# Normalizing entering chunks per node, between two turns, in place of two averaging products

## The chip, the cores and the metric

The kernel runs on one core of one Trainium2 chip. The metric is the device time of one execution in microseconds (us), the median of several runs. TensorE (PE) multiplies matrices, VectorE (DVE) and ScalarE (ACT) work on elements, GpSimd (POOL) adds and moves data, and SyncE (SP) starts most of the transfers. Each engine works through its own queue in order and waits for the others by semaphores.

## The reference

Four graph layers run one after another on x of shape 8 x 2048 x 64 (batch, nodes, features), each with the same frame:

```python
h = jnp.maximum(_layernorm(x, axis=-1), 0.0)
x = x + layer(h, adj, ...)
```

The layer norm takes mean and variance over the 64 features of one node, without learned weights, with 1e-5 added to the variance. The change concerns layers 2 and 3:

```python
# layer 2: node 0 of h is overwritten with intervention_value, then three steps of
effects = jnp.einsum('nm,bmd->bnd', adj_matrix, v)
h = jax.nn.relu(jnp.einsum('bnk,dk->bnd', jnp.concatenate([v, effects], -1), W1) + b1)
v = jnp.einsum('bnk,dk->bnd', h, W2) + b2
# layer 3: products of x with I, A and 2AA - I, then weights that differ by node
out = jnp.einsum('bnki,nkio->bno', x_g, w) + b     # w, b made from a 16-wide embedding of the node
```

All four layers share the 2048 x 2048 adjacency matrix of zeros and ones.

## The kernel before

The eight batches form four pairs. A pair's state is a tile of 128 partitions (two batches with 64 features each) by 2048 nodes, held in four chunks of 512 nodes. This is the layout with features on the partitions. After layer 1 the state of each pair waits in DRAM (`x2_dram`). Then `layers23` works off layers 2 and 3 pair by pair, with the transposed adjacency matrix resident in SBUF (`aT`).

**A pair's work.** Layer 2 has three steps, each of four chunks. In each, `spread` (L2092) multiplies the features by one chunk of columns of the adjacency matrix: 16 row blocks, two matmuls each, since every factor is held as two rounded parts (hi and lo). In the third step each chunk is handed to `leave` (L2128), which adds the result to the state and already makes the normalized input of layer 3. Layer 3 spreads twice. In its last loop over the chunks (L2240), each chunk's spread gives y2, and then come the products with the weights that differ by node. For each of the four row tiles of the chunk and each of two halves of the weights (w), six matmuls fill two PSUM tiles, u0 and u1. DVE multiplies both by the embedding (L2269), adds (L2273) and folds (L2280); POOL folds further (L2281, L2282), adds the state (L2283), and SP stores the result (L2284).

**The next pair enters during that loop.** While chunk c of layer 3 is worked on, chunk c-1 of the next pair is loaded, normalized and written over the part of v that is no longer needed. In the last chunk (c = 3, LAST) two chunks enter: c = 2, and c = 3, which is kept in columns of `y1` until v is free. `enter` (L2115) does this. It calls `normed` (L2077), sets node 0 to the intervention value if c is 0, and calls `moved` (L2048). That makes the first weighted features of the next pair: four products `py`, then a rounded copy hi on ACT and the remainder lo on DVE (L2062, L2063).

**How `normed` works before.** Features lie on partitions, so their mean is a product: `kit.avg` is a 128 x 128 matrix with 1/64 in two diagonal blocks, and `mm(mean, kit.avg, src)` puts the mean of each node on all of its 64 partitions. DVE subtracts (L2082), ACT squares (L2083), a second product `var` averages the squares, ACT takes Ln and Exp with -0.5 (L2087, L2088), and DVE does maximum and multiplication (L2089). Both are float32 products of 512 columns.

**How `leave` works before.** It turns a chunk with four 128 x 128 transposes on PE (`kit.turn`), so that nodes lie on partitions. ACT copies the PSUM tile back over xp (L2140). The 64 features of a node then lie in a row, and a reduce on DVE gives their sum (L2144). DVE subtracts the mean (L2146), ACT squares (L2147), DVE reduces (L2148), ACT takes Ln and Exp of eight numbers per partition (L2149, L2150), and DVE does maximum and multiplication (L2151). The result vn is used turned. Later four more transposes (`tv`) turn it back, and ACT copies it into v (L2163).

**What sets the order of the work.** All of PE's instructions in these layers stand in program order. The program order is woven by a small planner, `Weave`: `enter` and the like are generators that yield an estimate, in microseconds, of the delay until their next part is due. `weave.passed(t)` is called after each piece of the main work and runs the parts that have come due. A row block of a spread counts 0.47, a group of six products of u counts 2.8. The other engines' orders come from the framework's scheduler, which keeps data dependences. [...]the tags acc, tp, u0 and u1 have two each, used in turn. The entering chunks use u0 and u1 for their products, so these alternate with the main products' tiles.

```python
if xn is not None:
    weave.start(enter(c - 1, after, xn, 0.2, ("u0", "u1")))
    if c == LAST:
        weave.start(enter(c, after, xl, 0.6, ("u0", "u1"), y1))
spread(acc, yn, c, True, every)
```

Of the kernel before, what the change touches and what calls it, by code (L numbers as in the profile page):

```python
# [8 lines left out]
FP = mybir.dt.float32  # L9
FR = mybir.dt.float32r  # L10
AF = mybir.ActivationFunctionType
OP = mybir.AluOpType
AX = mybir.AxisListType
# [3 lines left out]
P = 128  # L17
B, N, F = 8, 2048, 64
# [3 lines left out]
CW = 512  # L22
# [9 lines left out]
def cols(c, w=CW):  # L32
    return slice(c * w, (c + 1) * w)
# [603 lines left out]
class Kit:  # L637
# [97 lines left out]
    def mm(self, *args, **kw):  # L735

        one = self.nc.tensor.matmul(*args, **kw)  # L737
        if self.strict:
            self.tc.keep_in_program_order(one)
# [1267 lines left out]
def layers23(self, aT):  # L2007
    kit, x2_dram, x3_dram, out, ctx, fin, v = (
        self.kit, self.x2_dram, self.x3_dram, self.out, self.ctx, self.fin, self.v
    )  # L2010
    tc, nc, t, mm = kit.tc, kit.nc, kit.t, kit.mm
# [5 lines left out]
    sb = ctx.enter_context(tc.tile_pool(name="f_sb", bufs=2, reuse_waits="tile"))  # L2017
    ps = ctx.enter_context(tc.tile_pool(name="f_ps", bufs=2, space=PSUM, reuse_waits="tile"))
# [21 lines left out]
    def parts(lent):  # L2040

        if lent:
            return [sb.tile([P, 4, P], FR, tag=lent[0], name=n, bufs=lent[1]) for n in ("hi", "lo")]
        return self.parts()
# [3 lines left out]
    def moved(v, c, W, bias, lent=None):  # L2048

        py = ps.tile([P, 4, P], FP, tag="tp", name="py")  # L2050
        for k in range(4):
            m = 4 * c + k
            mm(py[:, k, :], v[:, m * P : (m + 1) * P], W, start=True, stop=True)
        return in_parts(py, bias, lent)

    def in_parts(py, bias=None, lent=None):
        hi, lo = parts(lent)
        if bias is not None:
            yb = fin.tile([P, 4, P], FP, tag="ca", name="yb")
            nc.vector.tensor_tensor(yb, py, bias[:, None, :].to_broadcast([P, 4, P]), op=OP.add)  # L2060
            py = yb
        nc.scalar.copy(hi, py)  # L2062
        nc.vector.tensor_tensor(lo, py, hi.bitcast(FP), op=OP.subtract)  # L2063
        return hi, lo
# [9 lines left out]
        nc.vector.tensor_tensor(lo, tp, hi.bitcast(FP), op=OP.subtract)  # L2074
        return hi, lo

    def normed(dst, src, tags, xc=None):  # L2077

        mean = ps.tile([P, CW], FP, tag=tags[0], name="mean")
        mm(mean, kit.avg, src, start=True, stop=True)  # L2080
        xc = fin.tile([P, CW], FP, tag="ca", name="xc") if xc is None else xc
        nc.vector.tensor_sub(xc, src, mean)  # L2082
        nc.scalar.activation(dst, xc, AF.Square)  # L2083
        yield 3.0
        var = ps.tile([P, CW], FP, tag=tags[1], name="var")
        mm(var, kit.avg, dst, start=True, stop=True)
        nc.scalar.activation(dst, var, AF.Ln, bias=kit.eps)  # L2087
        nc.scalar.activation(dst, dst, AF.Exp, scale=-0.5)  # L2088
        nc.vector.scalar_tensor_tensor(dst, xc, 0.0, dst, op0=OP.max, op1=OP.mult)  # L2089
        yield 3.0  # L2090

    def spread(acc, y, c, start, ms):  # L2092

# [14 lines left out]
    def load(dst, src, c):  # L2108
        nc.sync.dma_start(out=dst, in_=src[:, cols(c)])
        return dst  # L2110

    def chunk_of(src, c):
        return load(fin.tile([P, CW], FP, tag="x", name="xp"), src, c)

    def enter(c, y, xp, delay, tags, at=None):  # L2115

        yield delay
        src, k = (v, c) if at is None else (at, 1)
        yield from normed(src[:, cols(k)], xp, tags, at if at is None else at[:, cols(2)])
        if c == 0:  # L2120
            nc.vector.tensor_copy(v[:, 0:1], ivc)
        y[c] = moved(src, k, W1e, None)

    def carry(c, step, yn):
# [3 lines left out]
    def leave(p, c, xp, yn):  # L2128

        yield 1.8 if c == LAST else 2.3  # L2130
        pv = ps.tile([P, CW], FP, tag="tp", name="pv")
        mm(pv, W2, v[:, cols(c)], start=True, stop=True)
        nc.vector.scalar_tensor_tensor(xp, pv, b2c, xp, op0=OP.add, op1=OP.add)
        bq = load(sb.tile([P, CW], FP, tag="pr", name="bq", bufs=3), kit.bias_dram, c)
        yield 1.8

        tx = ps.tile([P, 4, P], FP, tag="u0", name="tx")
        for k in range(4):
            kit.turn(tx[:, k, :], xp[:, k * P : (k + 1) * P])
        nc.scalar.copy(xp, tx.rearrange("p k n -> p (k n)"))  # L2140
        groups = lambda a: a.rearrange("p (g f) -> p g f", f=F)
        spans = lambda a: a[:, :, None].to_broadcast([P, 8, F])
        st = sb.tile([P, 2, 8], FP, tag="st", name="st")
        nc.vector.tensor_reduce(st[:, 0], groups(xp), AX.X, OP.add)  # L2144
        vn = fin.tile([P, CW], FP, tag="ca", name="vn")
        nc.vector.scalar_tensor_tensor(groups(vn), spans(st[:, 0]), -1.0 / F, groups(xp), op0=OP.mult, op1=OP.add)  # L2146
        nc.scalar.activation(v[:, cols(c)], vn, AF.Square)  # L2147
        nc.vector.tensor_reduce(st[:, 1], groups(v[:, cols(c)]), AX.X, OP.add)  # L2148
        nc.scalar.activation(st[:, 1], st[:, 1], AF.Ln, bias=kit.eps, scale=1.0 / F)  # L2149
        nc.scalar.activation(st[:, 1], st[:, 1], AF.Exp, scale=-0.5)  # L2150
        nc.vector.scalar_tensor_tensor(groups(vn), groups(vn), 0.0, spans(st[:, 1]), op0=OP.max, op1=OP.mult)  # L2151
        hi, lo = parts(LENT[c])
        flat = lambda a: a.rearrange("p k n -> p (k n)")
        nc.scalar.copy(flat(hi), vn)
        nc.vector.tensor_tensor(flat(lo), vn, flat(hi).bitcast(FP), op=OP.subtract)
        yn[c] = hi, lo
        nc.gpsimd.tensor_add(bq, bq, xp)  # L2157
        nc.sync.dma_start(out=x3_dram[p, :, cols(c)], in_=bq)
        yield 7.0
        tv = ps.tile([P, 4, P], FP, tag="u1", name="tv")  # L2160
        for k in range(4):
            kit.turn(tv[:, k, :], vn[:, k * P : (k + 1) * P])
        nc.scalar.copy(v[:, cols(c)], flat(tv))  # L2163

    def again(y1, c, yn):
        yield 1.4
# [22 lines left out]
    for p in range(NP):  # L2189
        for step in range(3):  # L2190
# [3 lines left out]
            for c in range(NCW):  # L2194
                if step == 0 or c % 2 == 0:
                    accs = [ps.tile([P, CW], FP, tag="acc", name="acc") for d in range(2 if step else 1)]
                acc = accs[c % 2 if step else 0]
                if step < 2:
                    got = raw(2)
                else:  # L2200
                    xp = chunk_of(x2_dram[p], c)
                if step == 0:
                    mm(acc, W1v, v[:, cols(c)], start=True, stop=False)
                    weave.passed(0.93)
                    spread(acc, y, c, False, every)
                elif c % 2 == 0:
                    spread(acc, y, c, True, range(0, 8))
                    quarters(accs, Wvc, c)
                    spread(acc, y, c, False, range(8, NT))
                else:  # L2210
                    spread(acc, y, c, False, every)
                b = b1c if step else b1
                if step < 2 and c % 2:
                    for h in range(2):
                        nc.scalar.activation(v[half(1 - h), cols(c)], acc[half(h)], AF.Relu, bias=b[half(h)])
                else:
                    nc.scalar.activation(v[:, cols(c)], acc, AF.Relu, bias=b)
                if step < 2:
                    check(got)
                weave.start(carry(c, step, yn) if step < 2 else leave(p, c, xp, yn))  # L2220
# [19 lines left out]
        for c in range(NCW):  # L2240
            xr = chunk_of(x3_dram[p], c)
            acc = ps.tile([P, CW], FP, tag="acc", name="acc")
# [4 lines that stand above are left out]
# [7 lines left out]
            for k in range(4):  # L2254
# [3 lines left out]
                for w in range(2):  # L2258
                    u = [ps.tile([P, 8, F], FP, tag=f"u{h}", name=f"u{h}") for h in range(2)]
                    for kk, src in enumerate((v[:, ns], y1[:, ns], y2[:, ks])):  # L2260
                        for h in range(2):
# [3 lines left out]
                                start=kk == 0, stop=kk == 2,  # L2265
                            )
                    for h in range(2):
                        a = sb.tile([P, 8, F], FP, tag="pr", name="pr", bufs=3)
# [125 lines left out]
```

## Time and profile before

| | us |
|---|---|
| median of 3 runs (1881.08 to 1883.15) | 1881.71 |
| the profiled execution | 1880.27 |
| its span, first to last instruction | 1878.1 |
| PE busy (98% of the span) | 1840.7 |
| DVE busy (63%) | 1174.5 |
| ACT busy (25%) | 463.1 |
| POOL busy (17%) | 311.7 |

The TensorE clock granted to the core was 0.996 of full speed. PE, DVE, ACT, POOL and SP are the engines, PEld is PE's loading of weights. A line of the timeline gives start, duration, engine, line of the kernel, operation, output <- inputs, shapes and the number of merged instructions; in brackets stands how long the engine was idle before, and what ended that. A float32 matmul shows as two records, so one mean product is x2 and the four products py are x8. Transposes carry line L744, and all other matmuls here L737, since two helpers issue them. The chain of work that ended last follows the end of the program back, at each step to what released it. The three changes of pair lie at 980 to 1076, 1246 to 1343 and 1513 to 1609 us in the span.

### The profile page before, as it was taken

What the parts mean: (1) busy time and instruction counts of PE and PEld (TensorE: products, weight loads), DVE (VectorE), ACT (ScalarE), POOL (GpSimd) and SP (SyncE); (2) the same over time, 40 slices, a digit from 0 to 9 for tenths busy, and PEclk for the clock granted to TensorE, in tenths of its full rate; (3) what the DMA queues carried; (4) which work ended last, traced back from release to release, by engine and by line L of the source; (5) the groups of instructions that cost most, each with busy time, mean ns of one, the idle gap of its engine ahead of it and who ended that gap; (6) DMA issues with size and microseconds to landing.
All of it is one profiled execution on the core that took longest, in us unless ns stands there. A gap on an engine that the chain in (4) does not pass through costs nothing.

```text
span 1878.1 us, 26150 instructions
## 1 busy us (share of the span) xinstructions
PE 1840.7 (98%) x10364; PEld 1146.9 (61%) x10364; DVE 1174.5 (63%) x1843; ACT 463.1 (25%) x1048; POOL 311.7 (17%) x435
## 2 busy tenths in 40 slices
PE   8999999899999999999999999999999999999997
PEld 7877767443333333577765577855677755777653
DVE  7766699789999999932446732357523275524465
ACT  5422455572222221121301112200112101113000
POOL 4211387220000000000111200012100021101122
PEclk9999999999999999999999999999999999999999
DMA  7666395383222222142101022101122011121000
GB/s 205 186 185 207 103 284 144 107 208 79 54 61 52 63 57 57 46 99 67 51 13 28 22 69 62 34 23 26 43 62 62 12 30 28 54 65 51 5 20 12
DMA packets 86372, 142.60 MB, mean 76 GB/s; under 512 B 33800, under 2 KB 34056, under 8 KB 83568
## 3 DMA queue, kind: packets, MB, share of 16 engines
q1 hardware_dynamic: 64976, 80.64, 14.8%
q0 software_dynamic: 21040, 56.98, 12.4%
q10 hardware_dynamic: 224, 3.22, 0.5%
q8 instruction: 83, 1.36, 0.3%
q14 instruction: 49, 0.40, 0.1%
HBM read 106.85 MB, written 37.09 MB: 77 GB/s over the span
## 4 chain that ended last, share of the span: by engine, by line
PE 50%; issue 10%; DMA 2%; POOL 2%; DVE 1%; POOLq 0%; ACT 0%; SPq 0%; DVEq 0%
PE acc L737 31%; PE u L737 14%; PE py L737 2%; PE pv L737 1%; POOL fold L2281 1%; PE var L737 1%; PE mean L737 1%; DMA xd<-e 0%; DMA W3f<-in_L_gnn_weight 0%; DMA den<-d_dram 0%; PE tx L744 0%; POOL ot L2282 0%; PE tv L744 0%; PE tp L744 0%; DVE pt L1807 0%
## 5 line engine op out<-in xcount | busy, mean ns | idle before, releaser
L737 PE MATMUL acc<-aT,parts 128*128 128x512 f32 x1664 | 441.3, 409 | 0.0
L737 PEld LDWEIGHTS acc<-aT,parts 128*128 128x128 f32 x1664 | 306.6, 188 | 97.7 <-issue 39.2
L737 PE MATMUL o<-pt,hS 128*32 128x512 f32 x2048 | 247.1, 593 | 2.0 <-DVE pt L632 1.2
L737 PE MATMUL u<-W3f,y 64*128 64x512 f32 x1024 | 241.3, 589 | 0.0
L2269 DVE TENSOR_TENSOR pr<-u,embf 128x512 f32<-128x512 f32 x256 | 170.6, 687 | 109.8 <-PE u L737 103.1
L1807 DVE SCALAR_TENSOR_TENSOR pt<-R,wd,aT 128x1024 f32<-128x1024 f32 x188 | 230.0, 1276 | 8.5 <-DMA R<-r_dram 5.2
L737 PEld LDWEIGHTS u<-W3f,y 64*128 64x128 f32 x1024 | 100.0, 187 | 119.8 <-issue 119.8
L737 PEld LDWEIGHTS o<-pt,hS 128*32 128x32 f32 x2048 | 79.1, 110 | 143.8 <-issue 112.8
L737 PE MATMUL dn<-pt,vd 128*32 128x512 f32 x1024 | 134.9, 593 | 0.0
L737 PE MATMUL u<-W3f,v 64*128 64x512 f32 x512 | 133.0, 596 | 0.0
L2281 POOL TENSOR_TENSOR fold<-fold 128x256 f32<-128x256 f32 x64 | 47.8, 746 | 495.8 <-DVE fold L2280 495.8
L2060 DVE TENSOR_TENSOR yb<-py,cb_f 128x512 f32<-128x512 f32 x32 | 22.1, 691 | 157.9 <-PE py L737 157.9
L1106 PE MATMUL acc<-at,Y 128*128 128x512 f32 x384 | 101.7, 405 | 0.3 <-ACT ev L1136 0.2
L737 PE MATMUL acc<-aTl,parts 128*128 128x512 f32 x384 | 99.7, 398 | 0.0
L2157 POOL TENSOR_TENSOR bq<-bq,xp 128x512 f32<-128x512 f32 x16 | 20.7, 1293 | 421.9 <-ACT xp L2140 421.9
L2273 DVE TENSOR_TENSOR pr<-pr 128x512 f32<-128x512 f32 x128 | 88.0, 688 | 2.2
L737 PEld LDWEIGHTS u<-W3f,v 64*128 64x128 f32 x512 | 56.5, 186 | 49.6 <-issue 36.3
L1807 DVE SCALAR_TENSOR_TENSOR pt<-R,wd,aTl 128x1024 f32<-128x1024 f32 x64 | 79.3, 1280 | 8.6 <-PE dn L737 3.9
L737 PEld LDWEIGHTS dn<-pt,vd 128*32 128x32 f32 x1024 | 40.7, 110 | 67.7 <-issue 49.2
L737 PEld LDWEIGHTS acc<-aTl,parts 128*128 128x128 f32 x384 | 71.5, 188 | 16.2
L1106 PEld LDWEIGHTS acc<-at,Y 128*128 128x128 f32 x384 | 68.5, 188 | 14.1 <-issue 0.8
L2074 DVE TENSOR_TENSOR parts<-tp,parts 128x512 fp32r<-128x512 f32 x16 | 11.1, 692 | 85.3 <-ACT parts L2073 85.3
(374 smaller groups left out, 2683.0 us busy)
## 6 DMA issues: line engine op xcount, KB each, us to landing
at<-in_adjT POOLq DMA_DIRECT2D x32, 512.0 KB, 4.6
raw<-in_adjT SPq DMA_DIRECT2D x64, 256.0 KB, 3.3
aT<-in_adjT POOLq DMA_DIRECT2D x12, 1024.0 KB, 7.5
xp<-xd SPq DMA_DIRECT2D x45, 256.0 KB, 2.9
R<-r_dram SPq DMA_DIRECT2D x14, 512.0 KB, 3.8
hhi<-hi_dram POOLq DMA_DIRECT2D x18, 235.1 KB, 4.3
hlo<-lo_dram POOLq DMA_DIRECT2D x18, 235.1 KB, 4.4
hi_dram<-hi SPq DMA_DIRECT2D x16, 264.0 KB, 3.1
```

The costliest lines, as they stand in the source:

```text
L737: one = self.nc.tensor.matmul(*args, **kw)
L1106: mm(acc[p], Y[h][:, m, p, :], at[:, k, :], start=m + h == 0, stop=m == NT - 1 and h == 1)
L1807: V.scalar_tensor_tensor(pt, R, w, a.bitcast(FP), op0=OP.max, op1=OP.mult)
L2060: nc.vector.tensor_tensor(yb, py, bias[:, None, :].to_broadcast([P, 4, P]), op=OP.add)
L2074: nc.vector.tensor_tensor(lo, tp, hi.bitcast(FP), op=OP.subtract)
L2157: nc.gpsimd.tensor_add(bq, bq, xp)
L2269: nc.vector.tensor_tensor(a, u[h], emb[:, i, 8 * w : 8 * w + 8, None].to_broadcast([P, 8, F]), op=OP.mult)
L2273: nc.vector.tensor_add(pr[h], pr[h], a)
L2281: nc.gpsimd.tensor_add(fold[:, :, 0:2, :], fold[:, :, 0:2, :], fold[:, :, 2:4, :])
```

## The change

The body of `leave` that turns and normalizes is moved into `normed`, and the turning back into `back`, both plain functions. `leave` calls them in place of the old lines, with the same instructions. `enter` calls them too, in place of the old `normed` with its two products.

```diff
-    def normed(dst, src, tags, xc=None):
-
-        mean = ps.tile([P, CW], FP, tag=tags[0], name="mean")
-        mm(mean, kit.avg, src, start=True, stop=True)
-        xc = fin.tile([P, CW], FP, tag="ca", name="xc") if xc is None else xc
-        nc.vector.tensor_sub(xc, src, mean)
-        nc.scalar.activation(dst, xc, AF.Square)
-        yield 3.0
-        var = ps.tile([P, CW], FP, tag=tags[1], name="var")
-        mm(var, kit.avg, dst, start=True, stop=True)
-        nc.scalar.activation(dst, var, AF.Ln, bias=kit.eps)
-        nc.scalar.activation(dst, dst, AF.Exp, scale=-0.5)
-        nc.vector.scalar_tensor_tensor(dst, xc, 0.0, dst, op0=OP.max, op1=OP.mult)
-        yield 3.0
+    def normed(xp, tag, vn, q):
+
+        tx = ps.tile([P, 4, P], FP, tag=tag, name="tx")
+        for k in range(4):
+            kit.turn(tx[:, k, :], xp[:, k * P : (k + 1) * P])
+        nc.scalar.copy(xp, tx.rearrange("p k n -> p (k n)"))
...
+        nc.vector.tensor_reduce(st[:, 0], groups(xp), AX.X, OP.add)
+        nc.vector.scalar_tensor_tensor(groups(vn), spans(st[:, 0]), -1.0 / F, groups(xp), op0=OP.mult, op1=OP.add)
+        nc.scalar.activation(q, vn, AF.Square)
+        nc.vector.tensor_reduce(st[:, 1], groups(q), AX.X, OP.add)
+        nc.scalar.activation(st[:, 1], st[:, 1], AF.Ln, bias=kit.eps, scale=1.0 / F)
+        nc.scalar.activation(st[:, 1], st[:, 1], AF.Exp, scale=-0.5)
+        nc.vector.scalar_tensor_tensor(groups(vn), groups(vn), 0.0, spans(st[:, 1]), op0=OP.max, op1=OP.mult)
+
+    def back(vn, dst, tag):
+
+        tv = ps.tile([P, 4, P], FP, tag=tag, name="tv")
+        for k in range(4):
+            kit.turn(tv[:, k, :], vn[:, k * P : (k + 1) * P])
+        nc.scalar.copy(dst, tv.rearrange("p k n -> p (k n)"))
...
     def enter(c, y, xp, delay, tags, at=None):
 
         yield delay
         src, k = (v, c) if at is None else (at, 1)
-        yield from normed(src[:, cols(k)], xp, tags, at if at is None else at[:, cols(2)])
+        vn = fin.tile([P, CW], FP, tag="ca", name="vn") if at is None else at[:, cols(2)]
+        normed(xp, tags[0], vn, src[:, cols(k)])
+        yield 7.0
+        back(vn, src[:, cols(k)], tags[1])
         if c == 0:
             nc.vector.tensor_copy(v[:, 0:1], ivc)
+        yield 1.4
         y[c] = moved(src, k, W1e, None)
```

The delays of `enter` change with it: before, 3.0 to the second product and 3.0 to `moved`; now 7.0 to the turning back and 1.4 to `moved`. In PE's order this puts tx where mean stood, removes var, puts the first tv behind the last row block of the spread, and puts py behind the first six products of u, where it stood ahead of the spread's last row block (or, for the second entry in LAST, behind it). In LAST the second entry's tv follows the first one's py, and its py follows the second six products.

More of the change, by code (lines that the diff above doesn't have):

```diff
@@ L2075, in turned @@
         return hi, lo
-    def normed(dst, src, tags, xc=None):
-        mean = ps.tile([P, CW], FP, tag=tags[0], name="mean")
-        mm(mean, kit.avg, src, start=True, stop=True)
-        xc = fin.tile([P, CW], FP, tag="ca", name="xc") if xc is None else xc
-        nc.vector.tensor_sub(xc, src, mean)
-        nc.scalar.activation(dst, xc, AF.Square)
-        yield 3.0
-        var = ps.tile([P, CW], FP, tag=tags[1], name="var")
-        mm(var, kit.avg, dst, start=True, stop=True)
-        nc.scalar.activation(dst, var, AF.Ln, bias=kit.eps)
-        nc.scalar.activation(dst, dst, AF.Exp, scale=-0.5)
-        nc.vector.scalar_tensor_tensor(dst, xc, 0.0, dst, op0=OP.max, op1=OP.mult)
-        yield 3.0
+    def normed(xp, tag, vn, q):
[3 more added lines that the diff above has]
+        nc.scalar.copy(xp, tx.rearrange("p k n -> p (k n)"))
+        groups = lambda a: a.rearrange("p (g f) -> p g f", f=F)
+        spans = lambda a: a[:, :, None].to_broadcast([P, 8, F])
+        st = sb.tile([P, 2, 8], FP, tag="st", name="st")
+        nc.vector.tensor_reduce(st[:, 0], groups(xp), AX.X, OP.add)
[10 more added lines that the diff above has]
+        nc.scalar.copy(dst, tv.rearrange("p k n -> p (k n)"))
     def spread(acc, y, c, start, ms):
@@ L2135, in leave @@
         yield 1.8
[L2137 to L2144, printed above, removed]
-        vn = fin.tile([P, CW], FP, tag="ca", name="vn")
[L2146 to L2151, printed above, removed]
+        vn = fin.tile([P, CW], FP, tag="ca", name="vn")
+        normed(xp, "u0", vn, v[:, cols(c)])
         hi, lo = parts(LENT[c])
@@ L2159, in leave @@
         yield 7.0
[L2160 to L2163, printed above, removed]
+        back(vn, v[:, cols(c)], "u1")
     def again(y1, c, yn):
```

## The prediction

> **What bounds the kernel now.** I read the profile's first part, then the chain of work that ended last, then the timeline of the entering chunks. The first part says that TensorE is busy all the time:
>
> ```profile
> PE 1840.7 (98%) x10364; PEld 1146.9 (61%) x10364; DVE 1174.5 (63%) x1843; ACT 463.1 (25%) x1048; POOL 311.7 (17%) x435
> ```
>
> Busy time alone proves little here, because a matmul lasts 409 ns by its record and the next one starts 232 ns later. The chain says more: from 976 us on, its long pieces are PE's own (acc, u, py, var, mean) and its issue time, with short tails of POOL (fold 1.2% of it). So in layers 2 and 3 a microsecond of PE slots is a microsecond of the end, as long as no operand is late. The slots are read as distances between starts. The timeline on PE has the entering chunk c=2 of the first pair, the LAST chunk (c=3, where two chunks enter), and two chunks of the last pair, in which nothing enters:
>
> ```profile
> 1011.65 0.73 PE L737 MATMUL acc<-aT,parts 128*128 128x512 f32 x2
> 1012.22 1.02 PE L737 MATMUL mean<-xp,avg_f 128*128 128x512 f32 x2
> ...
> 1016.28 1.06 PE L737 MATMUL var<-v,avg_f 128*128 128x512 f32 x2
> ...
> 1020.40 1.05 PE L737 MATMUL py<-W1e_f,v 128*128 128x128 f32 x8
> ...
> 1021.86 1.13 PE L737 MATMUL u<-W3f,v 64*128 64x512 f32 x4
> ...
> 1042.66 0.73 PE L737 MATMUL acc<-aT,parts 128*128 128x512 f32 x2
> ...
> 1076.24 1.13 PE L737 MATMUL acc<-v,W1v_f 128*128 128x512 f32 x2
> ...
> 1750.58 1.55 PE L737 MATMUL acc<-aT,parts 128*128 128x512 f32 x6
> ...
> 1779.29 5.74 PE L737 MATMUL acc<-aT,parts 128*128 128x512 f32 x24
> ...
> 1786.83 1.13 PE L737 MATMUL u<-W3f,v 64*128 64x512 f32 x4
> ...
> 1807.63 5.78 PE L737 MATMUL acc<-aT,parts 128*128 128x512 f32 x24
> ```
>
> A chunk with no guest takes 1807.63 - 1779.29 = 28.34 us (28.38 the next one): I take 28.36. With one guest it takes 1042.66 - 1011.65 = 31.01 us, so **one entering chunk costs 2.66 us** (31.02 - 28.36, c=1 having 31.02). LAST takes 1076.24 - 1042.66 = 33.58, so **two cost 5.21 us**. The other two pair changes repeat this (31.04 and 33.57 in the third). Of 2.66, py is 0.89 by the chain, so mean and var together are 1.77. One turn of a chunk (four transposes) is priced by the chunk from 1750.58 to 1779.29, which holds one (tp): 28.71 - 28.36 = **0.35 us**.
>
> The new chain has not run in these places, but it runs in the leaving chunks. From DVE, ACT and POOL on the timeline there:
>
> ```profile
> 897.00 0.69 DVE L2144 TENSOR_REDUCE st<-xp 128x8 f32<-128x512 f32 x1 [2.16 <-ACT xp L2140]
> 897.05 1.29 POOL L2157 TENSOR_TENSOR bq<-bq,xp 128x512 f32<-128x512 f32 x1 [81.79 <-ACT xp L2140]
> 897.72 1.17 DVE L2146 SCALAR_TENSOR_TENSOR vn<-st,xp 128x512 f32<-128x512 f32 x1
> 898.98 0.63 ACT L2147 ACTIVATE v<-vn 128x512 f32<-128x512 f32 x1 [2.02 <-DVE vn L2146]
> 899.64 0.69 DVE L2148 TENSOR_REDUCE st<-v 128x8 f32<-128x512 f32 x1 [0.76 <-ACT v L2147]
> 900.37 0.30 ACT L2149 ACTIVATE st<-st,eps_f 128x8 f32<-128x8 f32 x1
> 900.70 0.21 ACT L2150 ACTIVATE st<-st 128x8 f32<-128x8 f32 x1
> 900.94 0.69 DVE L2151 SCALAR_TENSOR_TENSOR vn<-vn,st 128x512 f32<-128x512 f32 x1 [0.61 <-ACT st L2150]
> ```
>
> From the first reduce to the end of vn this takes 4.63 us. And where DVE stands when an entering chunk begins (c=1, whose spread starts on PE at 980.63):
>
> ```profile
> 983.19 0.68 DVE L2273 TENSOR_TENSOR pr<-pr 128x512 f32<-128x512 f32 x1
> 983.79 0.68 DVE L2082 TENSOR_TENSOR xc<-xp,mean 128x512 f32<-128x512 f32 x1
> 984.39 0.42 DVE L2280 TENSOR_TENSOR fold<-pr 128x256 f32<-128x256 f32 x1
> 984.89 0.73 POOL L2281 TENSOR_TENSOR fold<-fold 128x256 f32<-128x256 f32 x1 [3.82 <-DVE fold L2280]
> ```
>
> DVE is still busy with the products of the chunk before for 3.2 us. The guest's first operation on DVE gets its turn 3.16 us after the spread began.
>
> **What the Trainium skill says.** SBUF — State Buffer, "Who interferes with whom": a VectorE instruction with two SBUF inputs contends with a GpSimd instruction that reads SBUF, and whichever started first keeps the shared ports for its whole length. The trace agrees with this: L2146 takes 1.17 us where L2151, of the same shape and also with two SBUF inputs, takes 0.69; POOL's bq add ran until 898.34, which is 0.62 into L2146, and 0.55 remain. All 16 of L2146 have this neighbour. VectorE: DVE Perf Modes, "The perf-mode tier table": tensor_reduce has only the 1x mode; the trace has 0.69 us for 512 elements, as dear as an add. TensorE: Matmul & The Clock Gate, "Part 4: PE-mode transpose": a 128x128 transpose lasts about 275 ns in a kernel; the records here say 272, but four of them hold up the stream only 0.35 us, so I use the spacing.
>
> **The change, part by part.** There are 12 entering chunks: three changes of pair, each with c=0 and 1 entering one at a time and c=2 and 3 together in LAST.
>
> Removed: mean and var, 1.77 us of PE in a single entry, subtraction and last multiply on DVE (0.68, 0.69), Square, Ln and Exp on ACT (0.63, 0.69, 0.63). Added: tx and tv on PE, 2 x 0.35 = 0.70; two copies of 0.59 and two tiny activations on ACT, which is busy for 25% of the span; two reduces on DVE. In the built program the order of SP and POOL is unchanged.
>
> Moved: py. It stood in the spread, two matmuls from its end; now it stands behind the first six products of u. There PE goes from products on half the rows to a full-array product and back. The first group of six takes 2.68 us after a spread and 2.57 later, and the last takes 2.67, so each crossing costs 0.10. py in the new place is 0.89 + 0.20 = 1.09. Its lower bound is 0.89 (the crossing hides behind weight loads). A single entry thus costs 0.70 + 1.09 = 1.79 in place of 2.66: **0.87 saved**. LAST costs 1.40 + 2.18 = 3.58 in place of 5.21: **1.63 saved** (its second tv shares py's crossing).
>
> New wait: tv stands right behind the spread and needs vn; every product of u is queued behind it, and DVE's multiplications behind those. PE gets there at 7.54 - 0.10 + 0.35 = 7.79 us after the spread began (7.54 is 1786.83 - 1779.29). DVE: reduce at 3.16 (in xc's place), fold at 3.76, L2146's subtraction at 4.09 (an add followed a fold 0.33 after its start). POOL's fold begins at 4.26 at the earliest, as in the fence, so the subtraction has the ports first and lasts 0.69. Then by the steps of the leaving chunk: Square 4.87, reduce 5.53, Ln 6.26, Exp 6.59, multiply 6.83 to 7.52. **0.27 before PE needs it: no wait.** If it lasts 1.17 all the same, vn is ready at 8.00 and PE waits 0.21.
>
> In LAST the two guests interleave on DVE: subtraction 4.09 to 4.78, second reduce to 5.38, second subtraction behind POOL's pushed-back fold (5.51) to 6.10, Square of the second on ACT to 6.8 ahead of the first's Ln, two reduces to 7.52, first vn 7.55 to 8.24. PE arrives at 7.44 + 0.70 = 8.14: a wait of **0.10**. With both subtractions at 1.17 vn comes at about 9.20: 1.06. The second tv also takes the u1 bank that alternates with the first products': 0.05.
>
> Late next, at no cost: lo of the entering chunk (0.69 on DVE) now lies among the products. In the single entry it falls into DVE's idle 1.29 us before the second group of products; in LAST, the second py's 1.09 on PE gives DVE the time. If that cover is gone, each costs up to 0.69. The freed xp buffer comes 0.9 us later, and its next load has a whole u stage of 20.8 us.
>
> Sum per pair change: 2 x 0.87 + 1.63 - 0.10 - 0.05 = 3.22; times 3 = **9.7 us**. The profiled execution took 1880.27 (span 1878.1 and 2.2 around it), which gives 1870.6; against the median of 1881.71 it gives **1872.0**. With turns at 0.44 (in the leaving chunk of the fence four transposes and six matmuls of 0.232 fill 1.83), 24 x 0.09 = 2.2 is lost; with py at 0.89, 12 x 0.20 = 2.4 is won.
>
> **The rivals.**
> - *The vn chain is late.* L2146 is slow by itself or POOL gets in first. For it: all 16 records say 1.17, never less. Against: the multiply L2151, of the same kind, takes 0.69 with POOL still. Waits of 0.21, 0.21 and 1.06 replace 0.10: 2 x 0.66 + 0.52 = 1.84, times 3 = 5.5; **1876.2**.
> - *lo is uncovered.* DVE needs 4.8 us of PE's 5.15 in each row tile, and waits on it only 0.35. If 12 times 0.69 came through, 8.3 would be given back: **1880.3**, no change. Against: py itself gives PE's side 1.09 each time.
> - *POOL's whole train goes first* (slower). POOL has three operations in a row there, 0.73 + 0.46 + 0.46, to 6.06. If the subtraction stands behind all of them, it ends at 6.61, vn at 9.35, in LAST at about 10.13; waits of 1.56, 1.56 and 1.99 against 3.32 saved: +1.79 per pair change, +5.4: **1887.1**. It decides if DVE's subtraction starts over 0.17 later than I put it, and it is a loss once the three waits pass 3.32. Against: DVE issues ahead, while POOL must be told that the fold is done.
>
> That the products stay is ruled out: the built order has no mean and var there.
>
> **How the numbers follow.** Forecast 0.58, late chain 0.24, lo 0.10, POOL first 0.08. The range runs from the cheap py (1869.6) to past the late chain with dearer turns (1876.2 + 1.7): 1869.6 to 1877.9, leaving out 0.18. Faster by over 0.2% (3.8 us, about what a measurement of this kernel can tell from no change) means below 1877.9: the first two, 0.82; within it, lo: 0.10; slower: 0.08.
>
> **What would show it.** Single-entry chunks of 30.15 us from spread to spread and LAST of 32.1; tx and tv of 0.35 each; the subtraction at 0.69 in entries and 1.17 in exits; POOL's fold lengthened instead; no PE wait before tv in single entries. It is wrong if PE stands before tv for over 0.3 us, if a gap opens in the u stage behind DVE, or if py's crossing is dearer than 0.2.

## The result, and the profile after

The median is 1875.83 us (1873.88 to 1877.00, seven runs) against 1882.46 for the kernel before (1880.53 to 1883.37, seven runs): a ratio of **0.9964 [0.9955, 0.9973]**, 6.6 us less. The forecast was 9.7 less. The profiled execution took 1875.95 (span 1874.1); the one before took 1880.27.

The first part of the page looks as it did, with TensorE busy all the time:

```profile
PE 1836.8 (98%) x10412; PEld 1150.6 (61%) x10412; DVE 1189.9 (63%) x1867; ACT 466.5 (25%) x1072; POOL 316.1 (17%) x435
```

The timeline of the kernel after on PE, from the spread of c=1 in the first pair to the end of LAST (start, length, engine, line, operation):

```profile
981.83 0.73 PE L737 MATMUL acc<-aT,parts 128*128 128x512 f32 x2
982.40 0.60 PE L744 MATMUL tx<-ident_f,xp 128*128 128x128 f32 x4
982.75 5.29 PE L737 MATMUL acc<-aT,parts 128*128 128x512 f32 x22
987.87 2.03 PE L737 MATMUL acc<-aTl,parts 128*128 128x512 f32 x8
989.74 0.60 PE L744 MATMUL tv<-ident_f,vn 128*128 128x128 f32 x4
990.27 1.13 PE L737 MATMUL u<-W3f,v 64*128 64x512 f32 x4
...
993.05 1.16 PE L737 MATMUL py<-W1e_f,v 128*128 128x128 f32 x8
994.13 1.13 PE L737 MATMUL u<-W3f,v 64*128 64x512 f32 x4
...
996.81 1.02 PE L737 MATMUL u<-W3f,v 64*128 64x512 f32 x4
...
1012.37 0.74 PE L737 MATMUL acc<-aT,parts 128*128 128x512 f32 x2
...
1042.91 0.73 PE L737 MATMUL acc<-aT,parts 128*128 128x512 f32 x2
...
1051.77 1.13 PE L737 MATMUL u<-W3f,v 64*128 64x512 f32 x4
...
1054.55 1.16 PE L737 MATMUL py<-W1e_f,v 128*128 128x128 f32 x8
1055.55 0.60 PE L744 MATMUL tv<-ident_f,y 128*128 128x128 f32 x4
1056.08 1.13 PE L737 MATMUL u<-W3f,v 64*128 64x512 f32 x4
...
1075.60 1.13 PE L737 MATMUL acc<-v,W1v_f 128*128 128x512 f32 x2
```

A chunk with one guest takes 30.54 us in place of 31.02, LAST 32.69 in place of 33.58. The whole stretch, from the first entering spread of a pair change to the products with W1v, took 95.61, 95.68 and 95.64 before; now it takes 93.77, 94.13 and 93.76. **Together that is 5.27 us less**, and this is the effect of the change as the traces show it: all that follows the first entering spread outside the three stretches takes 610.6 us in both. The medians say 6.6 with an interval of 5.1 to 8.5, which holds 5.27; whether the other 1.3 is more than scatter is not shown. The time ahead of the first entering spread scatters by more than that: it begins anywhere from 978.9 to 986.5 us in the profiles of this study (980.63 before, 981.83 after). So I compare stretches below, and medians beside them.

The new chain of the same guest, on DVE, ACT and POOL:

```profile
984.99 0.68 DVE L2086 TENSOR_REDUCE st<-xp 128x8 f32<-128x512 f32 x1
985.59 0.41 DVE L2277 TENSOR_TENSOR fold<-pr 128x256 f32<-128x256 f32 x1
985.92 0.68 DVE L2087 SCALAR_TENSOR_TENSOR vn<-st,xp 128x512 f32<-128x512 f32 x1
986.08 1.12 POOL L2278 TENSOR_TENSOR fold<-fold 128x256 f32<-128x256 f32 x1 [3.83 <-DVE fold L2277]
...
988.60 0.69 DVE L2092 SCALAR_TENSOR_TENSOR vn<-vn,st 128x512 f32<-128x512 f32 x1 [0.61 <-ACT st L2091]
989.51 0.59 PEld L744 LDWEIGHTS tv<-ident_f,vn 128*128 128x128 f32 x4
989.74 0.60 PE L744 MATMUL tv<-ident_f,vn 128*128 128x128 f32 x4
```

Counted from the spread's start at 981.83: reduce at 3.16, subtraction at 4.09 with 0.68 us, vn done at 7.46. PE starts tv at 7.91, with no idle time noted before it.

### The profile page after: what moved, and what is told of

It is laid out like the page before. It is cut to its first block, busy times and chain, and to the rows that moved or that the text cites. A ratio compares the mean times of both kernels' runs of the same rounds, so it can differ in the third digit from the quotient of the medians.

```text
span 1874.1 us, 26303 instructions
## 1 busy us (share of the span) xinstructions
PE 1836.8 (98%) x10412; PEld 1150.6 (61%) x10412; DVE 1189.9 (63%) x1867; ACT 466.5 (25%) x1072; POOL 316.1 (17%) x435
## 3 DMA queue, kind: packets, MB, share of 16 engines
q8 instruction: 84, 1.38, 0.3%
## 4 chain that ended last, share of the span: by engine, by line
PE 49%; issue 10%; DMA 2%; POOL 2%; DVE 1%; POOLq 0%; ACT 0%; SPq 0%; DVEq 0%
PE acc L737 31%; PE u L737 14%; PE py L737 2%; PE pv L737 1%; PE tx L744 1%; PE tv L744 1%; POOL fold L2278 1%; DMA xd<-e 0%; DMA den<-d_dram 0%; DMA W3f<-in_L_gnn_weight 0%; PE tp L744 0%; DMA d_dram<-ds 0%; POOL ot L2279 0%; DVE pt L1807 0%; POOL ot L2280 0%
## 5 line engine op out<-in xcount | busy, mean ns | idle before, releaser
L737 PE MATMUL acc<-aT,parts 128*128 128x512 f32 x1664 | 430.7, 404 | 0.0
L2082 ACT COPY xp<-tx 128x512 f32<-128x512 f32 x25 | 14.7, 588 | 203.3 <-PE tx L744 203.3
```

## The experiments

Edits are against the kernel after, unless it says otherwise. A ratio is to the kernel before, timed beside each run. "Stretch" is the mean of the three pair changes (95.65 before, 93.89 after); "chunks" are the three of the first pair change: the two single entries, then LAST (31.02, 31.01 and 33.58 before; 30.54, 30.54 and 32.69 after). A "crossing" is a change of PE between products on half the rows (u) and products on the full array.

**Is py dear because it stands among the products of u?** Two runs ask this from both sides. The first puts py of the kernel after into the spread of the next chunk:

```diff
         back(vn, src[:, cols(k)], tags[1])
...
-        yield 1.4
+        yield 23.0
         y[c] = moved(src, k, W1e, None)
```

> The changed kernel, with py of a single entry moved on from among the products of u into the next chunk's spread, and both py of LAST to the end of its products. If the shortfall is the crossing (py costs 1.30 us of PE among the products, 0.89 in a spread), a single-entry chunk falls from 30.54 to about 30.1 us counted with the py that moves on, LAST by 0.5 to 0.9, and the time is 3 to 5 us below the changed kernel's: ratio to the kernel before 0.994 to 0.995 in place of 0.9964. If the shortfall is a late vn, py's place doesn't matter and the ratio stays at 0.9964. If it is DVE's lo among the products, the time falls too, but gaps before u, and not py's own slot, vanish in the trace.

Measured: 1875.69, 0.9962 [0.9947, 0.9976]; stretch 93.49; chunks 29.22, 30.15 and 34.11. The second single takes 30.15 with the first one's py in its spread, against 30.54 with its own among u, so py is 0.4 cheaper there. LAST lost it again, and the 3 to 5 us that I had expected below the kernel after did not come. LAST now holds three py: the second single's in its spread, and its own two at the pair's end (1074.92 to 1076.81). Without the one that is not its own (some 0.92) it takes 33.19 against 32.69. The timeline of this run, behind the first six products of LAST, shows why:

```profile
1055.26 0.66 PE L744 MATMUL tv<-ident_f,y 128*128 128x128 f32 x4
1055.36 1.29 DVE L2266 TENSOR_TENSOR pr<-u,embf 128x512 f32<-128x512 f32 x2 [2.81 <-PE u L737]
...
1056.70 0.18 PEld L737 LDWEIGHTS u<-W3f,v 64*128 64x128 f32 x1 [0.56 <-DVE pr L2266]
```

The second tv takes one of the two PSUM tiles (banks) of u1, so the next products get the bank that the first six had filled, and wait 0.56 until DVE has read it. In the kernel after the first py stands there, and no wait is noted. The prediction priced this bank at 0.05; without py in front of it, it costs LAST at least the 0.5 between 33.19 and 32.69.

The second run puts py of the **kernel before** behind the spread, with the averaging products left as they were:

```diff
         if c == 0:
             nc.vector.tensor_copy(v[:, 0:1], ivc)
+        yield 2.4 if at is None else 4.0
         y[c] = moved(src, k, W1e, None)
```

> The kernel before, averaging products kept, with only py moved to where the change puts it (behind the first six products of u, in LAST the second behind the second six). Crossing theory: each py costs 0.4 us more than in the spread, 12 of them about 5 us: 1.0025 of the kernel before. Late-vn theory: nothing here is late, so 1.000. Uncovered lo: between 1.000 and 1.004, with DVE-released waits of PE in the u stage.

Measured: 1886.30, 1.0023 [1.0015, 1.0030]; chunks 31.44, 31.43 and 34.37, so 0.42, 0.42 and 0.79 more than before, stretch 97.25 (1.60 more). Moving py by itself is a loss of 0.4 each, 4.8 us in all.

**Is lo covered?** It is computed twice for entering chunks:

```diff
         hi, lo = in_parts(py, bias, lent)
+        if again:
+            nc.vector.tensor_tensor(lo, py, hi.bitcast(FP), op=OP.subtract)
...
-        y[c] = moved(src, k, W1e, None)
+        y[c] = moved(src, k, W1e, None, again=True)
```

> The changed kernel, with the remainder lo of each entering chunk computed twice: 12 more DVE operations of 0.69 us among the products of u. If lo is covered (my step), the time is that of the changed kernel within 1 us, ratio 0.996 to 0.997. If lo is uncovered, up to 12 x 0.69 = 8.3 us come on top: ratio about 1.001.

Measured: 1876.37, 0.9963 [0.9950, 0.9975]; stretch 93.74, as in the first and third pair change of the kernel after (93.77 and 93.76). Another 0.69 on DVE changes nothing, so the first 0.69 costs nothing either. The rival "lo is uncovered" falls.

**What made the subtraction 1.17 in leaving chunks?** POOL's add to bq moves to DVE:

```diff
-        nc.gpsimd.tensor_add(bq, bq, xp)
+        nc.vector.tensor_add(bq, bq, xp)
```

> The changed kernel, with the bias addition bq of leaving chunks on DVE in place of POOL. If POOL's read of SBUF holds the ports, the subtraction of the mean in leaving chunks falls from 1.17 us to 0.68, as in entering chunks, in all 16. If it is slow there for another reason, it stays at 1.17. The time should not move by over 2 us.

All subtractions of a kind in one line (count, then shortest, median and longest in ns), first of the kernel after, then of this run:

```profile
L2087 DVE SCALAR_TENSOR_TENSOR vn<-st,xp x25: 682/1162/1170, 898.9 to 1720.5; 128x512 f32<-128x512 f32 x25
```

```profile
L2087 DVE SCALAR_TENSOR_TENSOR vn<-st,xp x25: 682/684/687, 899.4 to 1720.6; 128x512 f32<-128x512 f32 x25
```

After, 9 entries take 0.68 and 16 exits 1.16; with POOL silent there all 25 take 0.68. (The second guest of LAST has another name in the profile; its three take 0.69 in both runs.) The wait is POOL's, as the Trainium skill's page SBUF — State Buffer, "Who interferes with whom", has it. The stretch stays at 93.77. The single run took 1878.23; its end, from the last pair's second chunk on, is 2.5 us longer than after, with PE busy for as long (85.4), and this is not explained.

**How close is vn?** Two runs move the two ends together: one computes the first reduce of entering chunks twice, the other asks for tv two row blocks earlier:

```diff
         nc.vector.tensor_reduce(st[:, 0], groups(xp), AX.X, OP.add)
+        if twice:
+            nc.vector.tensor_reduce(st[:, 0], groups(xp), AX.X, OP.add)
...
-        normed(xp, tags[0], vn, src[:, cols(k)])
+        normed(xp, tags[0], vn, src[:, cols(k)], twice=True)
```

> The changed kernel, with the first reduce of each entering chunk computed twice, so that the subtraction of the mean reaches DVE 0.6 us later and after POOL's fold has begun. If the shared port decides (my step), the subtraction now lasts about 1.0 us in place of 0.68, vn is ready about 0.9 us later (8.3 to 8.4 after the spread began), and PE waits 0.4 to 0.5 us before tv in single entries and about 1 us in LAST: 2 us per change of pair, 6 us in all, ratio about 0.9995. If POOL's whole train of three goes first, the subtraction lasts about 2 us and the kernel is slower than before. If the port plays no part, only the 0.6 us of the added reduce come on top: waits of 0.2 us in single entries.

```diff
-        yield 7.0
+        yield 6.0
         back(vn, src[:, cols(k)], tags[1])
```

> The changed kernel, with tv due one microsecond earlier, so that it stands ahead of the last two row blocks of the spread. By the trace of the changed kernel vn is ready 7.46 us after the spread began, and PE would be there at about 6.95: a wait of about 0.5 us in single entries, and 0.5 to 1 in LAST, where the second tv now stands in the spread as well. If vn had more slack than that, no PE wait shows and the time stays. Time: 1 to 4 us above the changed kernel's, ratio 0.997 to 0.999.

Measured for the doubled reduce: 1883.59, 1.0003 [0.9995, 1.0011]; chunks 31.02, 31.03 and 33.84 (0.48, 0.49 and 1.15 more). The whole gain of the change is gone for 0.68 us of DVE in each entry. Its timeline, in a chunk whose spread begins at 984.00:

```profile
988.25 0.74 POOL L2280 TENSOR_TENSOR fold<-fold 128x256 f32<-128x256 f32 x1 [3.83 <-DVE fold L2279]
988.80 0.73 DVE L2089 SCALAR_TENSOR_TENSOR vn<-st,xp 128x512 f32<-128x512 f32 x1
...
991.53 0.69 DVE L2094 SCALAR_TENSOR_TENSOR vn<-vn,st 128x512 f32<-128x512 f32 x1 [0.61 <-ACT st L2093]
992.34 0.42 PEld L744 LDWEIGHTS tv<-ident_f,vn 128*128 128x128 f32 x4 [0.72 <-PE acc L737]
992.37 0.63 PE L744 MATMUL tv<-ident_f,vn 128*128 128x128 f32 x4 [0.32 <-DVE vn L2094]
```

vn is done 8.22 after the spread's start, and tv starts 0.15 behind it, at 8.37. In the kernel after PE came at 7.91; the difference is 0.46, nearly all of what the chunk lost. By the same 0.15, vn at 7.46 had **0.30 of slack** there. In LAST of the kernel after, vn is done at 8.08 and tv starts at 8.33. In this run tv follows vn by 0.06 there, so LAST had some 0.20 of slack. I had expected the subtraction to take about 1.0, POOL being first; it took 0.73, because only 0.19 of POOL's fold was left.

Measured for the earlier tv: 1881.28, 0.9998 [0.9990, 1.0007]; chunks 31.19, 31.19 and 33.08, which is more than the 1 to 4 us of loss that I had expected. vn is done 7.46 after the spread's start, as after, and PE waits 0.47 for it in the first of them:

```profile
990.13 0.63 PE L744 MATMUL tv<-ident_f,vn 128*128 128x128 f32 x4 [0.47 <-DVE vn L2092]
```

The single chunk loses 0.65, so 0.18 beside the wait stays unexplained. A queue position half a microsecond too early is at least as dear as a chain that is half a microsecond too long.

**Can the crossings be had back?** With tv and py of the single entries both in the next spread:

```diff
-        yield 7.0
+        yield 30.2 if c < LAST - 1 else 7.0
```

> The changed kernel, with both tv and py of a single entry moved on into the next chunk's spread, LAST left as it is. If the shortfall is the price of turns and py at the crossings to and from u, a single entry costs 0.36 + 0.36 + 0.90 = 1.6 us of PE in place of 2.18, 0.5 to 0.6 saved in each of six, about 3.3 us: ratio to the kernel before about 0.9945 to 0.995. If a late vn were behind it, the saving would be the waits alone, and there are none in the trace of the changed kernel in single entries: no change.

Measured: 1879.27, 0.9984 [0.9976, 0.9993]; chunks 28.81, 31.88 and 34.04, stretch 94.8. A miss. The first chunk now holds one turn (tx) and nothing else:

```profile
978.86 0.73 PE L737 MATMUL acc<-aT,parts 128*128 128x512 f32 x2
979.43 0.60 PE L744 MATMUL tx<-ident_f,xp 128*128 128x128 f32 x4
...
1007.67 0.73 PE L737 MATMUL acc<-aT,parts 128*128 128x512 f32 x2
```

It takes 28.81 where an empty one takes 28.36, so **one turn costs 0.45**, not the forecast 0.35. In the next chunk tv stands in the spread too, but py of c=0 waits:

```profile
1011.76 0.68 DVE L2087 SCALAR_TENSOR_TENSOR vn<-st,xp 128x512 f32<-128x512 f32 x1
...
1012.36 0.15 DVE L2133 COPY v<-ivc_f 128x1 f32<-128x1 f32 x1
1012.56 0.97 PEld L737 LDWEIGHTS py<-W1e_f,v 128*128 128x128 f32 x8 [1.86 <-DVE v L2133]
1012.56 1.16 PE L737 MATMUL py<-W1e_f,v 128*128 128x128 f32 x8 [1.42 <-DVE v L2133]
```

The copy that puts node 0 into the entered chunk takes 0.15 us, but it is queued on DVE behind the last products' work and the next guest's reduce and subtraction. A small operation on a busy queue became the longest wait of PE that these stretches show, 1.4 us. The next variant also put both tv of LAST behind the first six products, in the banks of "tp" in place of u1, and both its py at the pair's end:

```diff
-        yield 7.0
-        back(vn, src[:, cols(k)], tags[1])
+        single = c < LAST - 1
+        yield 30.2 if single else 7.3
+        back(vn, src[:, cols(k)], tags[1] if single else "tp")
...
-        yield 1.4
+        yield 1.4 if single else 23.0
```

> As the run with tv and py of single entries in the next spread, and in LAST both tv behind the first six products in one crossing, in the banks of tp, and both py at the end of the products, where PE leaves u anyway. Crossing theory: LAST costs 0.5 to 0.7 us less than in the changed kernel, on top of 0.5 to 0.6 for each single entry: about 5 us below the changed kernel, ratio to the kernel before about 0.9935 to 0.9945. A late vn or DVE's lo as the cause: no gain over the changed kernel.

Measured: 1876.08, 0.9969 [0.9958, 0.9980]; chunks 28.81, 31.88 and 33.68, stretch 94.37. This misses the expectation too: the same wait in the second chunk, but LAST is better. So the last variant leaves tv where the kernel after has it, moves only py into the next spread, and keeps what helped LAST:

```diff
-        yield 7.0
-        back(vn, src[:, cols(k)], tags[1])
+        single = c < LAST - 1
+        yield 7.0 if single else 7.3
+        back(vn, src[:, cols(k)], tags[1] if single else "tp")
...
-        yield 1.4
+        yield 23.0
```

> Single entries as in the run with py in the next spread (tv stays at the spread's end, so that the copy of node 0 is done long before py), LAST as in the run with fewer crossings. If PE's crossings are the cause and nothing waits, the stretch from the first entering spread to the next pair takes 92.6 us in place of 93.8 (the kernel before: 95.6), three times 1.2 or 3.5 us below the changed kernel: ratio to the kernel before about 0.9945. If the gain is lost in a wait again, as in the run before this one, the stretch stays above 93.5.

Measured: **1872.82, 0.9943 [0.9928, 0.9959]**, the lowest median of all; chunks 29.25, 30.15 and 33.27, stretch 92.65, 1.1 to 1.5 below the kernel after in each pair. (The two intervals of the medians overlap; the stretches tell the kernels apart.) The chunks repeat the prices: two turns cost 29.25 - 28.36 = 0.89, and a py in a spread 30.15 - 29.25 = 0.90. On its timeline LAST begins with one py in the spread, has both tv behind the first six products, no wait on u1, and both py at the end:

```profile
1043.20 0.73 PE L737 MATMUL acc<-aT,parts 128*128 128x512 f32 x2
...
1055.33 0.66 PE L744 MATMUL tv<-ident_f,vn 128*128 128x128 f32 x4
1055.82 0.60 PE L744 MATMUL tv<-ident_f,y 128*128 128x128 f32 x4
1056.35 1.13 PE L737 MATMUL u<-W3f,v 64*128 64x512 f32 x4
...
1075.58 1.06 PE L737 MATMUL py<-W1e_f,y 128*128 128x128 f32 x8
1076.47 1.02 PE L737 MATMUL acc<-v,W1v_f 128*128 128x512 f32 x2
```

The kernel after, run again:

> The changed kernel once more, beside the others on one chip, for direct comparison: 0.9955 to 0.9973 of the kernel before by every theory.

Measured: 1874.73, 0.9963 [0.9950, 0.9977]; stretches 93.77, 94.12 and 93.76, the same three as the first time to 0.01.

## Why the prediction was right, and where its sizes were off

The mechanism held: PE slots are the bound, the averaging products leave, turns come in, and nothing new waits. The median alone does not say so: 1875.83 lies nearer to the late-chain rival's 1876.2 than to the forecast 1872.0. The traces decide between them, with no wait before tv. The forecast of 9.7 was too high, and two terms of the sum account for nearly all of it. Costs on PE beyond an empty chunk, in us:

| term | forecast | measured | from |
|---|---|---|---|
| a turn (tx or tv) | 0.35 | 0.45 | spread to u 8.44 against 7.54 empty: 0.90 for two; LAST 8.86: 1.32 for three; one alone: 0.45 |
| py among u | 1.09 | 1.30 | u stage 22.10 against 20.80 |
| single entry | 1.79 | 2.18 | 30.54 - 28.36 |
| waits in LAST | 0.15 | none seen | timeline |
| LAST | 3.73 | 4.33 | 32.69 - 28.36 |

Per pair change 2 x 0.39 + 0.60 = 1.38 of the forecast saving is missing, 4.1 in three, and 0.35 more in one chunk (below): 9.7 - 4.5 = 5.2, against 5.27 measured.

- **The turn.** The step that failed is "28.71 - 28.36 = 0.35". Its two chunks don't begin alike. The one at 1750.58 follows another spread, and its second matmul starts 0.23 behind the first; the empty one follows products of u, where the second starts 0.33 behind, 0.10 for the crossing. Against 28.26 the turn is 0.45, as the chunk with one turn shows. The dear bound, 0.44, was right. The Trainium skill's TensorE: Matmul & The Clock Gate, "Part 4: PE-mode transpose", gives about 275 ns for one transpose, and the records still agree (272 ns); but that is not the price. Four of them take 0.45 from the stream: 0.35 from their first start to the next matmul's, and the matmul behind that starts 0.32 later in place of 0.23.
- **py.** "Each crossing costs 0.10", two of them. The distance from py to the next u is 1.08 (993.05 to 994.13), which looks like the 1.09 of the forecast. That is chance: the forecast took its 0.20 from the groups beside py. The distance holds 0.20 over 0.89 already, and the groups on both sides lose 0.10 as well: 990.27 to 993.05 is 2.78 where a first group took 2.68, and the next takes 2.68 where a later one took 2.57. A visit to the full array costs 0.40 over py's own price, not 0.20; the move alone (0.42, 0.42, 0.79 for two) and the way back (0.4) say the same. The cheap bound of 0.89 is excluded. That "py's crossing is dearer than 0.2" was one of the prediction's signs of being wrong, and it came true.
- **The chain of vn.** Right: subtraction at 4.09 as forecast, 0.68 for 0.69, vn at 7.46 for 7.52, no wait. POOL's fold went from 0.73 to 1.12 in its place. The slack of 0.30 looks like the forecast 0.27, but that left out the 0.15 from vn's end to tv's start; PE's later arrival (7.91 for 7.79) and an earlier vn made up for it. The price of losing the slack is real (2.1 us and 1.7 us in the first pair change of two runs). The late chain and POOL's train in front are out for this kernel: POOL began 0.16 behind the subtraction in the nine entries above, and 0.04 behind it for LAST's second guest. That is close.
- **LAST.** Its second tv shares py's crossing, as forecast: py and tv together take 1.53 (1054.55 to 1056.08), 0.44 more than py alone. PE came to tv later than thought (8.33 for 8.14, with two dearer turns in front) and vn was earlier (8.08 for 8.24), so 0.10 of wait vanished; on u1 no wait is noted.
- **lo.** Covered, shown by doubling it.

Open: in the first chunk of the second pair change u takes 0.35 longer than elsewhere, in both runs of the kernel after and in none of their other pair changes. From 1263.75 on the two halves of u run out of step until the chunk's end, with the usual 2.57 from group to group; the last group then takes 3.03 in place of 2.68. With tv earlier the same chunk has it (31.55 for 31.19), and with tv and py in the next spread one LAST (34.37 for 34.04). What pushed the halves apart I did not find.

## What to carry to other kernels

Price an operation in a tuned stream by the difference of two stretches whose neighbours on both sides are alike, and count what the groups before and after it lose; its own start-to-start distance is only part. When two averaging products become two transposes, the gain is decided by where the rest can stand: put full-array work among full-array work, and check which small operation (a copy of one column, a bank's reader) is queued late on the engine that frees it. A chain that "just fits" should be tested by lengthening it: here 0.30 us of slack in six places and some 0.20 in three held up the whole gain.

## What the runs showed of the hardware that was not expected

- A DVE subtraction that started while POOL worked lasted the overlap plus some 0.55 us: 0.62 of POOL left gave 1.17 before, and 0.19 and 0.26 left gave 0.73 and 0.80 with the doubled reduce. The wait is for the neighbour's rest, not a fixed 0.5.
- Two half-array streams that were pushed apart stayed apart, and paid once, at the end. In the first run the seven groups of u from the 0.56 wait on u1 took 19.08 us in place of some 18.2. In between they kept their 2.57 from group to group; 0.44 was lost in the group of the wait and 0.41 in the last one. The open case above shows the same: only the last group is longer, by 0.35.
